# Key norms from the diagonal of k kᵀ, and a triangular substitution on GpSimd instead of VectorE

## The chip, the cores and the metric

The kernel runs on one core of a Trainium2 chip. The metric is the device time of one execution in microseconds (us); the time of a kernel is the median of several runs. A core has five engines with a queue of instructions each: TensorE (PE, with its weight loads shown apart as PEld), VectorE (DVE), ScalarE (ACT), GpSimd (POOL) and SyncE (SP), which here only issues DMAs. SBUF is the on-chip memory with 128 partitions; PSUM is the accumulator memory that TensorE writes.

## The reference

One transformer block with adaptive layer norm, for 8 sequences of 256 tokens with 256 channels. In order: a normalised and modulated input `h`; a gated delta-rule attention with 16 key heads of 128 channels, two value heads for each key head; a gated residual; and a feed-forward layer that keeps the two largest of every four hidden values. What matters here is the attention:

```python
qkv = einsum('btc,dc->btd', x, W_qkv)                 # then a causal convolution over 4 tokens
q = _l2norm(q); k = _l2norm(k)                        # k / sqrt(sum(k*k))
def step(S, inp):                                     # over the 256 tokens
    Sk = einsum('bhi,bhipj->bhpj', k_t, S)
    dv = b_t[..., None] * (v_t - Sk)
    S = S * d_t + einsum('bhi,bhpj->bhipj', k_t, dv)
    o = einsum('bhi,bhipj->bhpj', q_t, S)
```

The recurrence is computed in chunks of 128 tokens. Within a chunk the updates `dv` solve a triangular system whose matrix has the entries k_s·k_t times decay and beta, so the kernel needs the products k kᵀ of a chunk, the squared norms of the keys, and the inverse of a unit triangular 128x128 matrix for each value head and chunk.

## The kernel before

The work is ordered in 16 groups: four pairs of sequences, and in each four groups of four key heads (`groups`, `GH = 4`). While the four heads of one group go through `attend`, the next group is got ready in the background.

For each key head of the coming group `stage_a` makes: the keys `k_t` (two projections on TensorE into `ps_k`, then `convolved`: one ScalarE copy and six VectorE multiply-adds); the squared norms `n2` (`norms2`, line 499: four TensorE transposes of 128x128 into `ps_n2k`, line 447, and four ScalarE squares with a running sum, line 451); from them `rk2` and `bk` on VectorE, and `diag` and `nk` on GpSimd (lines 516 and 523); the products k kᵀ of four chunks into the PSUM bank `ps_kk` (line 532); a scan `e` over 1032 decay entries on VectorE (line 551); and the matrix `a_t` = `ps_kk` times `e` (line 563, two VectorE instructions of 512 elements). The 32x32 diagonal blocks of `a_t` go to DRAM in four DMAs (line 572).

When the four heads of a group are there, `stage_b` loads all their 128 blocks of 32x32 into `blk`, one block in each partition (line 585), and inverts them by substitution: 30 steps of two instructions, a product `tmp` (line 604) and a subtraction from `blk` (line 610), of j·(31−j) elements in step j. Each instruction needs the result of the one before. After step 16 and at the end ScalarE turns the result (lines 592 and 597), which goes to DRAM as `scr_x` and `scr_y`. `levels` loads it again (line 690 and after) and joins the blocks in four rounds of small matmuls (lines 707, 710, 720, 723, 737 to 751) to the 128x128 inverses `t_inv` that `attend` multiplies with (line 804).

`attend` ends with the norm of the output: `ss` on VectorE (line 858), `rs` by a power on GpSimd (line 105), four products `og` (line 871). In the background there are also units of the feed-forward layer, whose selection of two in four is VectorE work (lines 211 to 229).

The order of the instructions on each engine is fixed when the program is built, by a planner that plays the program through with costs of its own and puts on each engine what is ready, in the order in which the code gives it. On the chip each engine then takes its own list strictly in order. `tc.issue_after(ins)` puts the instructions of its block behind `ins` if they run on the same engine; the first group's heads are put behind the last instruction of the first substitution (`first_solved`, lines 1068, 1100 and 1134).

PSUM has eight banks here: three for `ps_in`, two for `ps_inv` (`ps_kk`, the rounds of `levels`, the feed-forward) and three for `ps_mix`.

Of the kernel before, what the change touches and what calls it, by code (L numbers as in the profile page):

```python
# [11 lines left out]
F32 = mybir.dt.float32  # L12
AF = mybir.ActivationFunctionType
ALU = mybir.AluOpType
AX = mybir.AxisListType
# [3 lines left out]
P = 128  # L19
# [29 lines left out]
def adaln_block(  # L49
# [18 lines left out]
    nc = tc.nc  # L68
# [4 lines left out]
    NCH = T // P  # L73
    NK = w_heads.shape[0]
    NV = 2 * NK
    NS = 2 * NCH
# [19 lines left out]
    ident = identx[:, 1:PE1]  # L96
# [269 lines left out]
    with ExitStack() as scope:  # L366
        rec_pool = scope.enter_context(tc.tile_pool(name="rec", bufs=7))
# [73 lines left out]
        def norms2(src, name):  # L441

            n2 = small.tile([P, 2, NCH], F32, tag=name, name=name)
            ps = bank(ps_in if name == "n2k" else ps_in, [P, 2, NCH, P], f"ps_{name}")
            for i in range(2):
                for n in range(NCH):
                    nc.tensor.transpose(ps[:, i, n, :], src[:, i, n * P : (n + 1) * P], ident)
            for i in range(2):
                for n in range(NCH):
                    junk = mixp.tile([P, P], F32, tag="junk", name="junk", bufs=2)  # L450
                    nc.scalar.activation(
                        junk, ps[:, i, n, :], AF.Square, accum_out=n2[:, i, n : n + 1]
                    )
            return n2
# [24 lines left out]
        def stage_a(kh, bp, hp, wk, h_bp, scr):  # L479

            rec = {"kh": kh, "bp": bp, "hp": hp, "h": h_bp}
            first = bp == 0 and kh < GH
            if not first:
                dbc = single.tile([P, 2, NS * PE1], F32, tag="dbc", name="dbc")
                nc.sync.dma_start(
                    out=dbc,
                    in_=d_dram[bp][kh]
# [3 lines left out]
            k_t = rec_pool.tile([P, 2, T], F32, tag="k_t", name="k_t")  # L491
# [4 lines left out]
            else:  # L496
                convolved(k_t, ps, conv_sb[:, kh, 0, :])
            yield rec
            n2 = norms2(k_t, "n2k")
            nc.vector.tensor_scalar_max(n2, n2, L2_EPS2)  # L500
            nk = small.tile([P, 2 * NCH], F32, tag="nk", name="nk", bufs=7)
            rec["nk"] = nk
# [22 lines left out]

            e = rec_pool.tile([P, 2, NS, PE1], F32, tag="e", name="e")
            rec["e"] = e
            ps_kk = bank(ps_inv, [P, 2 * NCH, P], "ps_kk")
            for i in range(2):
                for n in range(NCH):  # L530
                    kc = k_t[:, i, n * P : (n + 1) * P]
                    nc.tensor.matmul(ps_kk[:, i * NCH + n, :], lhsT=kc, rhs=kc, start=True, stop=True)
            if first:
                e_f, diag_f = e.rearrange("p i s t -> p (i s t)"), diag.rearrange("p s t -> p (s t)")
                for c0 in range(0, 2 * NS, 3):
# [26 lines left out]
            for i in range(2):  # L562
                nc.vector.tensor_tensor(
                    out=a_t[:, i].rearrange("p (n h) t -> p n h t", h=2),
                    in0=ps_kk[:, i * NCH : (i + 1) * NCH, None, :].to_broadcast([P, NCH, 2, P]),
                    in1=e[:, i, :, 0:P].rearrange("p (n h) t -> p n h t", h=2),
                    op=ALU.mult,
                )
# [8 lines left out]
        def stage_b(scr, scr_x, scr_y):  # L577

            blk = single.tile([P, Q, Q], F32, tag="blk", name="blk")
            nc.sync.dma_start(out=blk, in_=scr)
            xb = single.tile([P, Q, Q], F32, tag="xb", name="xb")
            nc.gpsimd.memset(blk.rearrange("p a b -> p (a b)")[:, :: Q + 1], -1.0)
            yield

            def turn(rows):  # L590

                nc.scalar.activation(
                    xb[:, rows], blk[:, :, rows].rearrange("p b a -> p a b"), AF.Copy, scale=-1.0
                )
                if rows.stop == Q:
                    nc.sync.dma_start(out=scr_x, in_=xb)
                nc.scalar.activation(blk[:, :, rows], blk[:, :, rows], AF.Copy, scale=-1.0)
                if rows.stop == Q:
                    nc.sync.dma_start(out=scr_y, in_=blk)

            for j in range(1, Q - 1):
                m = Q - 1 - j
                tmp = single.tile([P, j, m], F32, tag="tmp", name="tmp", bufs=2)
                nc.vector.tensor_tensor(  # L604
                    out=tmp,
                    in0=blk[:, j, None, j + 1 :].to_broadcast([P, j, m]),
                    in1=blk[:, 0:j, j, None].to_broadcast([P, j, m]),
                    op=ALU.mult,
                )
                solved = nc.vector.tensor_tensor(  # L610
                    out=blk[:, 0:j, j + 1 :], in0=blk[:, 0:j, j + 1 :], in1=tmp, op=ALU.subtract
                )
# [601 lines left out]
```

## Time and profile before

| | |
|---|---|
| median of 3 runs | 2111.28 us (2106.41 to 2114.01) |
| the profiled execution | 2106.59 us, of which the span from first to last instruction is 2104.6 us |
| TensorE busy | 2000.5 us, 95% of the span |
| VectorE busy | 1666.0 us, 79% |
| ScalarE busy | 1271.3 us, 60% |
| GpSimd busy | 391.1 us, 19% |
| mean granted TensorE clock | 0.991 |

The profile is that of one execution. A group line names the code line, the engine and the operation, the output and the inputs by the program's names, the shapes and the count; then come the total busy time in us, the mean duration of one in ns, and the time in which the engine sat idle just before these instructions, with what ended that idle time. A line of waits reads "who waited <- for whom: us in total, times, longest". Windows give for a stretch of the execution the busy time of each engine. A timeline line starts with the start and the duration in us.

### The profile page before, as it was taken

To read this page: it belongs to the slowest core of one execution; us is meant where nothing else is said; L and a number is where in the kernel's file an instruction comes from. 1 tells how busy PE (TensorE), PEld (TensorE's weight loads), DVE (VectorE), ACT (ScalarE), POOL (GpSimd) and SP (SyncE) were. 2 spreads that over 40 slices of the span, in tenths; PEclk is the share of its full clock that TensorE was granted. 3 is DMA by queue.
4 is the path that set the end of the run, shared out by engine and by line. 5 is a ranking of instruction groups with operands and counts; after the bars stand their busy time and mean duration, and the time that the engine had idled before them with its cause. 6 is when DMAs were issued, how large, how long until landed. Compare 5 with 4: busy or idle time off the path is not lost. (4 is left out here: it accounts for less than half of the span.)

```text
span 2104.6 us, 45727 instructions
## 1 busy us (share of the span) xinstructions
PE 2000.5 (95%) x16684; PEld 1583.3 (75%) x16684; DVE 1666.0 (79%) x4039; ACT 1271.3 (60%) x4260; POOL 391.1 (19%) x376
## 2 busy tenths in 40 slices
PE   8999999899999999999999989999999999999998
PEld 5567777677778777777777777777777877777877
DVE  6778887878788787788878779787978869787557
ACT  3557677766656556566665655657566655656652
POOL 3121312112121211212021121211213121121110
PEclk9999999999999999999999999999999999999999
DMA  4342414333343544434444443443444343344226
GB/s 127 99 131 72 117 55 108 99 80 105 92 115 103 125 115 102 123 105 111 140 92 111 107 123 113 114 115 99 128 110 115 97 127 110 94 121 116 66 91 218
DMA packets 356257, 230.99 MB, mean 110 GB/s; under 512 B 286265, under 2 KB 297913, under 8 KB 356033
## 3 DMA queue, kind: packets, MB, share of 16 engines
q1 hardware_dynamic: 336160, 167.53, 30.7%
q10 hardware_dynamic: 19872, 60.54, 9.3%
q8 instruction: 132, 2.16, 0.4%
q14 instruction: 93, 0.75, 0.1%
HBM read 188.38 MB, written 29.12 MB: 103 GB/s over the span
## 5 line engine op out<-in xcount | busy, mean ns | idle before, releaser
L420 DVE SCALAR_TENSOR_TENSOR cv<-ps_qv,conv_sb,cv 128x510 f32<-128x510 f32 (+2 forms) x564 | 409.4, 739 | 88.1 <-ACT cv L418 84.4
L432 PE MATMUL ps_qv<-h_bp,wh 128*128 128x512 f32 x768 | 365.7, 602 | 8.4 <-DVE cv L420 7.1
L105 POOL TENSOR_TENSOR rs<-ss,minus_halves 128x4 f32<-128x4 f32 x128 | 147.9, 1163 | 942.3 <-DVE ss L858 941.8
L646 PE MATMUL ps_z<-wh,h_bp 128*128 128x256 f32 x1024 | 252.1, 387 | 17.7 <-DVE cv L420 17.2
L901 PE MATMUL ps_y<-wo,og_p 128*128 128x256 f32 x1024 | 236.3, 380 | 2.6 <-ACT gz L653 2.2
L646 PEld LDWEIGHTS ps_z<-wh,h_bp 128*128 128x128 f32 x1024 | 186.9, 193 | 49.1 <-DVE cv L420 22.4
L838 ACT ACTIVATE junk<-o 128x128 f32<-128x128 f32 x512 | 154.2, 305 | 112.1 <-DVE o L854 96.8
L432 PEld LDWEIGHTS ps_qv<-h_bp,wh 128*128 128x128 f32 x768 | 134.3, 193 | 112.7 <-issue 100.2
L901 PEld LDWEIGHTS ps_y<-wo,og_p 128*128 128x128 f32 x1024 | 188.2, 190 | 27.7 <-ACT gz L653 3.3
L604 DVE TENSOR_TENSOR tmp<-blk 128x30 f32<-128x30 f32 (+14 forms) x480 | 156.9, 327 | 56.4 <-DMA blk<-scr 48.7
L418 ACT ACTIVATE cv<-ps_qv,conv_sb 128x512 f32<-128x512 f32 x188 | 129.3, 689 | 107.5 <-PE ps_qv L432 106.8
L516 POOL TENSOR_TENSOR diag<-consts,bk 128x1032 f32<-128x1032 f32 x64 | 123.5, 1929 | 364.5 <-DVE bk L507 329.1
L420 DVE SCALAR_TENSOR_TENSOR k_t<-ps_k,conv_sb,k_t 128x510 f32<-128x510 f32 (+1 forms) x189 | 139.8, 741 | 37.6 <-ACT k_t L418 35.6
L610 DVE TENSOR_TENSOR blk<-blk,tmp 128x30 f32<-128x30 f32 (+14 forms) x480 | 156.8, 327 | 9.6
L551 DVE TENSOR_TENSOR_SCAN e<-dbc,diag 128x1032 f32<-128x1032 f32 x60 | 138.1, 2302 | 19.5 <-POOL diag L516 13.4
L871 DVE SCALAR_TENSOR_TENSOR og<-o,rs,gz 128x128 f32<-128x128 f32 x512 | 145.8, 344 | 8.4 <-POOL rs L105 7.7
L812 PE MATMUL ps_ks<-u,cross 128*128 128x128 f32 x1024 | 141.7, 280 | 7.1 <-ACT u L806 3.9
L812 PEld LDWEIGHTS ps_ks<-u,cross 128*128 128x128 f32 x1024 | 128.7, 193 | 16.6 <-issue 6.3
L190 PE MATMUL ps_ff<-h,w_ff 128*128 128x128 f32 x1024 | 132.5, 277 | 4.2 <-ACT h L149 2.3
L190 PEld LDWEIGHTS ps_ff<-h,w_ff 128*128 128x128 f32 x1024 | 124.4, 192 | 14.9 <-issue 5.9
L778 ACT ACTIVATE vn<-ps_v,nk 128x256 f32<-128x256 f32 x256 | 104.5, 486 | 51.4 <-PE ps_v L773 51.2
L826 ACT ACTIVATE o<-ps_ks,g_in 128x128 f32<-128x128 f32 x256 | 79.9, 365 | 87.2 <-DVE rr L817 78.5
(180 smaller groups left out, 4189.9 us busy)
## 6 DMA issues: line engine op xcount, KB each, us to landing
wh<-in_w_heads ACTq DMA_DIRECT2D x64, 640.0 KB, 4.5
w_ff<-in_w_ff SPq DMA_DIRECT2D x128, 256.0 KB, 3.1
dbc<-d_dram SPq DMA_DIRECT2D x60, 516.0 KB, 3.7
wo<-in_w_heads ACTq DMA_DIRECT2D x32, 512.0 KB, 3.7
w_dn<-in_w_down SPq DMA_DIRECT2D x64, 256.0 KB, 3.0
wk<-in_w_keys SPq DMA_DIRECT2D x16, 512.0 KB, 3.5
scr<-a_t SPq DMA_DIRECT2D x256, 32.0 KB, 2.1
blk<-scr SPq DMA_DIRECT2D x16, 512.0 KB, 4.5
```

The costliest lines, as they stand in the source:

```text
L105: nc.gpsimd.tensor_tensor(out=out, in0=in_, in1=minus_halves[:, :n], op=ALU.pow)
L190: nc.tensor.matmul(ps[:, a, l, :], lhsT=w[:, k, l, :], rhs=h2[:, k, :], start=(k == 0), stop=(k == CC - 1),)
L420: nc.vector.scalar_tensor_tensor(out=dst[:, :, d:], in0=ps[:, :, : T - d], scalar=taps[:, KC - 1 - d : KC - d], in1=dst[:, :, d:], op0=ALU ...
L432: nc.tensor.matmul(ps.rearrange("p b t -> p (b t)"), lhsT=w[k], rhs=h_bp[:, k, :], start=(k == 0), stop=(k == CC - 1),)
L551: nc.vector.tensor_tensor_scan(e.rearrange("p i s t -> p (i s t)"), dbc.rearrange("p i f -> p (i f)"), diag.rearrange("p s t -> p (s t)"), ...
L604: nc.vector.tensor_tensor(out=tmp, in0=blk[:, j, None, j + 1 :].to_broadcast([P, j, m]), in1=blk[:, 0:j, j, None].to_broadcast([P, j, m]), ...
L610: solved = nc.vector.tensor_tensor(out=blk[:, 0:j, j + 1 :], in0=blk[:, 0:j, j + 1 :], in1=tmp, op=ALU.subtract)
L646: nc.tensor.matmul(ps[:, n, :], lhsT=h_bp[:, k, i * T + n * P : i * T + (n + 1) * P], rhs=wh[:, k * 640 + 384 : (k + 1) * 640], start=(k = ...
L812: nc.tensor.matmul(ps_ks[:, ct, h, :], lhsT=cross[:, h, ct, :], rhs=u0[:, h, :], start=True, stop=True)
L838: nc.scalar.activation(junk, o[:, n, h, :], AF.Square, accum_out=ss[:, n, h : h + 1])
L871: nc.vector.scalar_tensor_tensor(out=og[:, n, h, :], in0=o[:, n, h, :], scalar=rs[:, 2 * n + h : 2 * n + h + 1], in1=gz[:, i, n, h, :], op ...
L901: nc.tensor.matmul(ps_y[:, n, :], lhsT=og_p[:, j // 2, i, n, j % 2, :], rhs=wo[:, j // 2, j % 2, :], start=(j == 0), stop=(j == 3),)
```

## The change

Three parts, all in the background work:

- The squared norms of the keys are read from the diagonal of k kᵀ. The four products into `ps_kk` are made right behind the keys; ScalarE copies all of `ps_kk` to SBUF (`kk`, the odd half of the tile `a_t`, 512 elements for each partition); VectorE multiplies it with the identity into the even half and sums each row of 128 by a `tensor_reduce`. The four transposes and four squares for each key head fall away.
- `a_t` is then made from `kk` in SBUF instead of from PSUM, as two instructions by value head instead of by sequence, still 512 elements each. The second one writes over `kk` itself.
- The 60 instructions of each substitution run on GpSimd instead of VectorE. With that `first_solved` is a GpSimd instruction.

```diff
@@ stage_a
-            n2 = norms2(k_t, "n2k")
+            ps_kk = bank(ps_inv, [P, 2 * NCH, P], "ps_kk")
+            for i in range(2):
+                for n in range(NCH):
+                    kc = k_t[:, i, n * P : (n + 1) * P]
+                    nc.tensor.matmul(ps_kk[:, i * NCH + n, :], lhsT=kc, rhs=kc, start=True, stop=True)
+            a_t = rec_pool.tile([P, 2, NS, P], F32, tag="a_t", name="a_t", bufs=6)
+            rec["a"] = a_t
+            a_h = a_t.rearrange("p i (n h) t -> p (i n) h t", h=2)
+            kk, diagonal = a_h[:, :, 1], a_h[:, :, 0]
+            nc.scalar.copy(kk, ps_kk)
+            n2 = small.tile([P, 2, NCH], F32, tag="n2k", name="n2k")
+            nc.vector.tensor_tensor(
+                out=diagonal, in0=kk, in1=ident[:, None, :].to_broadcast([P, 2 * NCH, P]), op=ALU.mult
+            )
+            nc.vector.tensor_reduce(
+                out=n2.rearrange("p i n -> p (i n)"), in_=diagonal, axis=AX.X, op=ALU.add
+            )
...
-            ps_kk = bank(ps_inv, [P, 2 * NCH, P], "ps_kk")
...
-            a_t = rec_pool.tile([P, 2, NS, P], F32, tag="a_t", name="a_t", bufs=6)
-            rec["a"] = a_t
-            for i in range(2):
-                nc.vector.tensor_tensor(
-                    out=a_t[:, i].rearrange("p (n h) t -> p n h t", h=2),
-                    in0=ps_kk[:, i * NCH : (i + 1) * NCH, None, :].to_broadcast([P, NCH, 2, P]),
-                    in1=e[:, i, :, 0:P].rearrange("p (n h) t -> p n h t", h=2),
-                    op=ALU.mult,
-                )
+            e_h = e[:, :, :, 0:P].rearrange("p i (n h) t -> p (i n) h t", h=2)
+            for h in range(2):
+                nc.vector.tensor_tensor(out=a_h[:, :, h], in0=kk, in1=e_h[:, :, h], op=ALU.mult)
@@ stage_b
-                nc.vector.tensor_tensor(
+                nc.gpsimd.tensor_tensor(
                     out=tmp,
...
-                solved = nc.vector.tensor_tensor(
+                solved = nc.gpsimd.tensor_tensor(
                     out=blk[:, 0:j, j + 1 :], in0=blk[:, 0:j, j + 1 :], in1=tmp, op=ALU.subtract
```

More of the change, by code (lines that the diff above doesn't have):

```diff
@@ L527, in stage_a @@
             rec["e"] = e
-            ps_kk = bank(ps_inv, [P, 2 * NCH, P], "ps_kk")
-            for i in range(2):
-                for n in range(NCH):
-                    kc = k_t[:, i, n * P : (n + 1) * P]
-                    nc.tensor.matmul(ps_kk[:, i * NCH + n, :], lhsT=kc, rhs=kc, start=True, stop=True)
             if first:
@@ L559, in stage_a @@
             yield rec
-            a_t = rec_pool.tile([P, 2, NS, P], F32, tag="a_t", name="a_t", bufs=6)
-            rec["a"] = a_t
-            for i in range(2):
-                nc.vector.tensor_tensor(
-                    out=a_t[:, i].rearrange("p (n h) t -> p n h t", h=2),
-                    in0=ps_kk[:, i * NCH : (i + 1) * NCH, None, :].to_broadcast([P, NCH, 2, P]),
-                    in1=e[:, i, :, 0:P].rearrange("p (n h) t -> p n h t", h=2),
-                    op=ALU.mult,
-                )
+            e_h = e[:, :, :, 0:P].rearrange("p i (n h) t -> p (i n) h t", h=2)
+            for h in range(2):
+                nc.vector.tensor_tensor(out=a_h[:, :, h], in0=kk, in1=e_h[:, :, h], op=ALU.mult)
             a_f = a_t.rearrange("p i s t -> p (i s) t")
```

## The prediction

> **What bounds the kernel now.** I read the page's busy table first, then windows along one group, then the groups by shape, the waits, and the timeline around the substitution.
>
> ```profile
> PE 2000.5 (95%) x16684; PEld 1583.3 (75%) x16684; DVE 1666.0 (79%) x4039; ACT 1271.3 (60%) x4260; POOL 391.1 (19%) x376
> ...
> L604 DVE TENSOR_TENSOR tmp<-blk 128x30 f32<-128x30 f32 (+14 forms) x480 | 156.9, 327 | 56.4 <-DMA blk<-scr 48.7
> ...
> L610 DVE TENSOR_TENSOR blk<-blk,tmp 128x30 f32<-128x30 f32 (+14 forms) x480 | 156.8, 327 | 9.6
> ```
>
> TensorE is busy for all but 104 us of the span: it is the bound on the whole. The substitution (L604, L610) is 314 us of VectorE. One group of 122.6 us in the middle, cut into before, during and after its substitution (columns: sum, then PE, PEld, DVE, ACT, POOL busy):
>
> ```profile
> 1086.60:1128.80 42.20, 41.48 (x373) 32.63 (x372) 35.62 (x68) 25.17 (x95) 14.40 (x11) 1.00 0.51 134
> 1128.80:1170.60 41.80, 38.53 (x265) 32.23 (x264) 40.40 (x125) 23.94 (x82) 6.09 (x7) 1.00 0.32 92
> 1170.60:1209.20 38.60, 38.60 (x372) 29.04 (x372) 24.37 (x52) 25.52 (x79) 5.12 (x5) 1.00 0.47 119
> ```
>
> The middle row is the point: during the substitution VectorE is full (40.4 of 41.8) and TensorE loses 3.3 us, most of what it loses in the group. The list of waits agrees:
>
> ```profile
> DVE tmp L604 <- DMA blk<-scr: 48.7, 16, 7.0
> ...
> PE ps_z L646 <- DVE cv L420: 17.2, 15, 3.0
> ...
> PE ps_qv L432 <- DVE cv L420: 7.1, 7, 2.5
> PE ps_w L707 <- DMA x_even<-scr_x: 3.2, 3, 2.0
> ```
>
> VectorE stands 3 us a group in front of L604 until `blk` lands, and TensorE waits 24.3 us in all for convolutions that VectorE brings late. For the result of the substitution (`x_even`) it hardly waits.
>
> **The norms.**
>
> ```profile
> L451 ACT ACTIVATE junk<-ps_n2k 128x128 f32<-128x128 f32 x256 | 69.3, 289 | 60.4 <-PE ps_n2k L447 60.3
> ...
> L563 DVE TENSOR_TENSOR a_t<-ps_kk,e 128x512 f32<-128x512 f32 x128 | 81.9, 681 | 0.6
> ...
> L447 PE MATMUL ps_n2k<-consts,k_t 128*128 128x128 f32 x256 | 39.2, 276 | 1.2 <-ACT k_t L418 0.9 <-DVE k_t L420 0.3
> ```
> ```profile
> 1202.27 0.60 PE L447 MATMUL ps_n2k<-consts,k_t 128*128 128x128 f32 x4
> ```
>
> Four transposes take 0.60 us, one alone 0.276, so one more takes (0.60−0.276)/3 = 0.108 us of TensorE. 256 of them removed is 27.6 us at the pitch, 39.2 us by busy time. TensorE being the bound, I take 27.6 in full. ScalarE drops 256 squares (69 us and their accumulator reads) and gains 64 copies of 512 elements at about 0.69 us (as L418), 44 us: no bound before or after. VectorE gains a product (0.68, as L563) and a row sum, which no row shows; a copy of 512 elements from PSUM takes 0.679 us (L910), and I bound the sum by 0.4 (the 256-element statistics of L131) and 2.3 us (the 1032-element scan L551) and take 0.68, since cost here goes by elements read. 64 x 1.36 = 87 us against 314 us that leave: VectorE ends near 1440 us, 68%. In the chain from keys to `diag` 1.36 us of VectorE and a copy of 0.7 us replace four squares of some 0.29: under 1 us later for each head, covered by 40 us of other background work. `a_t` from SBUF keeps 512 elements; L169, both inputs in SBUF, takes 421 ns for 256, and PSUM-fed L198 413, so 0 us. `ps_kk` gives its bank back after the copy instead of after the scan, which can only help `levels` and the feed-forward; 0 to −5 us, I take 0. `a_t` is held from the norms on; six buffers, and the earlier hold is a scan long, 0.
>
> **The substitution on GpSimd.** No row shows it there; the nearest are these.
>
> ```profile
> L516 POOL TENSOR_TENSOR diag<-consts,bk 128x1032 f32<-128x1032 f32 x64 | 123.5, 1929 | 364.5 <-DVE bk L507 329.1 <-DVE e L551 11.1 <-DVE mv L132 10.4
> ...
> L657 POOL TENSOR_SCALAR eps_q<-n2q 128x4 f32<-128x4 f32 x64 | 24.8, 387 | 70.4 <-ACT junk L451 66.9
> ...
> L1012 POOL TENSOR_TENSOR taps<-consts,conv_sb 128x512 f32<-128x512 f32 x1 | 1.0, 1041 | 4.3 <-DMA conv_sb<-in_conv_w 4.3
> ```
>
> Undisturbed, L516 takes 1.917 us. With L1012 that gives 1.685 ns an element and 0.18 us fixed. The 30 steps have sum j(31−j) = 4960 elements, twice: 9920 x 1.685 ns + 60 x 0.18 = 27.4 us. A dependent instruction starts 0.04 us (VectorE's steps) to 0.1 us (`ss` to `rs`) after its source: +2.4 to +6, so 30 to 33; with L657's mean 0.387 as the fixed part it is 45. Into the same queue come 4 `rs` (1.16 each) and 2 `eps_q`: 5.4 us.
>
> Then the two engines disturb each other:
>
> ```profile
> 1363.39 2.48 DVE L229 SCALAR_TENSOR_TENSOR hid<-mag,hid 128x384 f32<-128x384 f32 x2
> ```
> ```profile
> 1363.58 2.14 POOL L516 TENSOR_TENSOR diag<-consts,bk 128x1032 f32<-128x1032 f32 x1 [3.87 <-DVE bk L507]
> ```
> ```profile
> L871 DVE SCALAR_TENSOR_TENSOR og<-o,rs,gz x512: 318/344/353, 137.0 to 2044.0; 128x128 f32<-128x128 f32 x171
> ```
>
> A VectorE instruction with both tensors in SBUF stood until `diag` was through (the quickest L229 takes 0.27), and `diag` itself started its data 0.22 us late behind the first. `og`, beside `rs` in many places, never exceeds 353 ns, so four-element powers hold nothing. In the window above the timeline has 40 such VectorE instructions besides the substitution, 13.9 us. GpSimd meets one in a third of cases for half of 0.35 us: 60 x 0.33 x 0.17 = 3.4 us. VectorE loses 40 x 0.75 x 0.14 = 4 us and has 19.7 us freed. So: 33 + 5.4 + 3.4 = 42 us against 41.8 now. The result is there when it is now; ends 36 and 54. I take 0, since L516 and L1012 are the same operation and L657 is another. What VectorE no longer does late is worth half of TensorE's 24.3 us: −12 (ends 0 and −24).
>
> Two rules of the Trainium skill speak against the change. "GPSIMD Engine Reference", Elementwise — side-by-side cycle accounting, has 2.6 cycles an element at 1.2 GHz, 2.17 ns where the rows give 1.685; by it the substitution is an estimated 4.8 us longer a group and the kernel near 2140. "SBUF — State Buffer", Who interferes with whom, lets whoever is first hold the shared port for the whole instruction; L516 agrees and L871 beside `rs` doesn't, and by the rule VectorE would lose an estimated 7 us a group instead of 4.
>
> **Start.** The first substitution runs undisturbed now, from 60.6 to 83.8 us, 23.2 us; on GpSimd 30 to 36 (45 at the outside). But the first heads' VectorE work, which line 1100 queued behind it, is now free of it. Ends 0 and +13, I take +5. `eps_q` of the first heads does queue behind it; `ss`, its only reader, comes after `levels` anyway.
>
> **Sum.** 2106.6 (the profiled execution) − 27.6 − 12 + 5 = 2072. Its time is 4.7 us under the median of 2111.3, so 2077.
>
> **Rivals.**
> Slower, the substitution arrives late. TensorE's order is fixed, and it comes to L707 just as `x_even` lands:
>
> ```profile
> 1174.74 1.82 SPq L690 DMA_DIRECT2D x_even<-scr_x  x4
> ```
> ```profile
> 1177.67 0.24 PE L707 MATMUL ps_w<-x_even,a_t 32*32 32x32 f32 x2
> ```
>
> 2.9 us with 2.3 us to landing (the DMA's median) leave 0.6 us. Every us that the planner does not know of costs 15 us over the groups; also the 3 us late `blk`, which VectorE absorbs now, would reach TensorE here. From 0.6 + 34/15 = 2.9 us a group the gain is gone. At 54 us instead of 42, half of it unplanned, it is (6−0.6) x 15 = 81 us: 2158. Against it: 12 waits of `og` for `rs` in 128 say that GpSimd's times are planned about right.
> Less: VectorE's port losses eat the relief, −12 becomes 0: 2089.
> No change: `t_inv` is used within about 4 us of being made, so the chain keys, substitution, `levels`, `attend` may set the 122 us and TensorE's saved time turns into idle time: 2111.
>
> **How the numbers follow.** Forecast 0.46, less 0.07, no change 0.07, late substitution 0.40. What can be told from no change is about 0.3%, 6 us. Faster is 0.46 + 0.07 = 0.53, same 0.07, slower 0.40. The likeliest case by itself spans 2047 (39.2 and 24 saved, nothing at the start) to 2097. The range takes in 2158 and a little more, leaving out the longer substitutions.
>
> **What would show it.** Right: TensorE's busy time falls by 28 to 39 us, the transposes of `ps_n2k` are gone, GpSimd's substitution pairs average near 0.46 us, VectorE in that stretch drops under 30 of 42 us, waits for DVE `cv` shrink, L707 still hardly waits. Wrong: L707 or L804 waits for `x_even` or ScalarE's `t_inv` by several us a group, or substitution instructions above 0.6 us.

## The result, and the profile after

The change makes the kernel slower. Median 2194.53 us (2193.74 to 2196.92, four runs) against 2112.65 us for the kernel before in the same session: a ratio of 1.0395, 95% interval 1.0371 to 1.0419. (A ratio here can differ by 0.1% from the quotient of the two medians.) The forecast was 2077 us, with a range to 2165; the sign is wrong and the time is outside the range. The profiled execution took 2196.92 us with a span of 2195.1.

From the page of the changed kernel, the busy times and three of the costliest groups (columns as before):

```profile
PE 2024.9 (92%) x16428; PEld 1589.9 (72%) x16428; DVE 1572.9 (72%) x3207; ACT 1245.7 (57%) x3813; POOL 882.9 (40%) x1336
...
L615 POOL TENSOR_TENSOR blk<-blk,tmp 128x30 f32<-128x30 f32 (+14 forms) x480 | 256.1, 534 | 35.4
L609 POOL TENSOR_TENSOR tmp<-blk 128x30 f32<-128x30 f32 (+14 forms) x480 | 244.7, 510 | 34.9 <-issue 0.2
...
L876 DVE SCALAR_TENSOR_TENSOR og<-o,rs,gz 128x128 f32<-128x128 f32 x512 | 193.3, 437 | 82.6 <-POOL rs L105 81.9
```

256 transposes are gone (16684 TensorE instructions have become 16428), and yet TensorE is busy for 24 us longer and idle for 2195.1 − 2024.9 = 170 us instead of 104. VectorE has 93 us less to do. Neither engine with less work has made the kernel faster.

The same cut of one group in the middle as before the change: the 42.2 us ahead of a substitution, the substitution, and 38.6 us behind it (columns: sum, then PE, PEld, DVE, ACT, POOL busy, the granted clock, the DMA share and GB/s).

```profile
1133.40:1175.60 42.20, 39.01 (x366) 29.13 (x365) 35.17 (x65) 22.38 (x71) 12.51 (x12) 0.96 0.53 144
1175.60:1218.20 42.60, 38.16 (x234) 32.49 (x233) 28.72 (x64) 20.95 (x75) 36.50 (x67) 0.96 0.25 78
1218.20:1256.80 38.60, 36.49 (x352) 27.52 (x351) 24.29 (x48) 25.98 (x74) 2.43 (x3) 0.96 0.46 114
```

In the middle row VectorE has fallen from 40.4 us to 28.7, and the substitution takes 42.6 us where it took 41.8. But in the first row, where the norms are made, VectorE has what it had before (35.2 us), and TensorE now loses 3.2 us there instead of 0.7, 4.4 instead of 3.3 in the middle and 2.1 instead of none behind. The granted clock, 1.00 in all three rows before, is 0.96.

The waits, in the order of the list (who waits <- for whom: us in total, times, longest):

```profile
DVE cv L420 <- ACT cv L418: 145.8, 50, 8.1
...
DVE og L876 <- POOL rs L105: 81.9, 38, 7.2
ACT xb L597 <- POOL blk L615: 76.3, 26, 9.9
...
PE ps_u L809 <- DVE aq L799: 34.4, 24, 3.8
...
PE ps_w L712 <- DMA x_even<-scr_x: 19.1, 11, 4.1
...
PE ps_kq L790 <- DVE o L859: 17.4, 6, 4.5
...
PE ps_qv L432 <- DVE cv L420: 9.8, 4, 3.1
```

In the kernel before, the first three were these; `xb` then waited for VectorE's last steps:

```profile
DVE cv L420 <- ACT cv L418: 84.4, 46, 4.5
...
ACT xb L592 <- DVE blk L610: 13.0, 8, 3.4
...
DVE og L871 <- POOL rs L105: 7.7, 12, 1.2
```

TensorE waits for `aq` and `o`, VectorE's steps inside `attend`, 52 us in all (4.2 before), where it used to wait for convolutions.

Where the 90.5 us between the two spans lie can be added up. The trace records every stretch in which TensorE was granted half its clock: 38 us within the span before, 147 us after, so 19 and 73 us of full-speed time lost, of which 17.6 and 67.9 lie in TensorE's busy time. TensorE's busy time at full clock is then 2000.5 − 17.6 = 1982.9 before and 2024.9 − 67.9 = 1957.0 after. So: 25.9 us of work saved, 66.1 us of idle time and 50.3 us of half clock added: +90.5. The idle time and the half clock are the large terms. The work is known less well: the runs below with the same 16428 TensorE instructions come out between 1944 us (d4) and 1978 (n1) by this reckoning.

One place shows how both arise. VectorE in the changed kernel (timeline: start, duration, then the instruction):

```profile
1152.91 0.69 DVE L573 TENSOR_TENSOR a_t<-a_t,e 128x512 f32<-128x512 f32 x1
...
1153.58 0.69 DVE L510 TENSOR_TENSOR a_t<-a_t,consts 128x512 f32<-128x512 f32 x1
1154.18 0.69 DVE L573 TENSOR_TENSOR a_t<-a_t,e 128x512 f32<-128x512 f32 x1
...
1155.10 0.68 DVE L513 TENSOR_REDUCE n2k<-a_t 128x4 f32<-128x512 f32 x1
...
1155.90 0.74 DVE L420 SCALAR_TENSOR_TENSOR cv<-ps_qv,conv_sb,cv 128x510 f32<-128x510 f32 x1
...
1157.41 0.68 DVE L799 TENSOR_TENSOR aq<-ps_kq,e 128x512 f32<-128x512 f32 x1
```

and TensorE there:

```profile
1151.91 1.88 PE L432 MATMUL ps_qv<-h_bp,wh 128*128 128x512 f32 x4
...
1158.15 0.74 PE L809 MATMUL ps_u<-vn,t_inv 128*128 128x128 f32 x4 [3.04 <-DVE aq L799]
1158.70 3.58 PE L432 MATMUL ps_qv<-h_bp,wh 128*128 128x512 f32 x4
```

The products that `aq` reads were through at 1152.1 us. `aq` runs at 1157.4, and VectorE, busy nearly all the while, takes the new product (L510) and row sum (L513) among others before it. TensorE, in its fixed order, waits 3.04 us. Then it pays again: four products of 512 columns that took 1.88 us before the gap take 3.58 us after it. Windows over the same place:

```profile
1136.00:1155.00 19.00, 18.85 (x220) 14.94 (x220) 18.33 (x35) 10.27 (x33) 8.07 (x8) 1.00 0.57 156
1155.00:1158.30 3.30, 0.26 (x3) 0.15 (x2) 3.27 (x9) 0.37 (x1) 0.66 (x1) 1.00 0.36 69
1158.30:1161.60 3.30, 3.30 (x8) 1.74 (x9) 3.30 (x4) 0.37 (x1) 2.23 (x2) 0.56 0.25 50
1161.60:1165.00 3.40, 3.40 (x19) 2.62 (x17) 3.31 (x6) 1.75 (x5) 0.00 (x0) 0.93 0.47 143
```

VectorE is full in all four rows (18.3 of 19.0 us, then 9.9 of 10.0), and the clock falls to 0.56 in the row behind the gap.

### The profile page after: what moved, and what is told of

Its sections match the earlier page's. It is cut to its first block, busy times and chain, and to the rows that moved or that the text cites. A ratio compares the mean times of both kernels' runs of the same rounds, so it can differ in the third digit from the quotient of the medians.

```text
span 2195.1 us, 44788 instructions
## 1 busy us (share of the span) xinstructions
PE 2024.9 (92%) x16428; PEld 1589.9 (72%) x16428; DVE 1572.9 (72%) x3207; ACT 1245.7 (57%) x3813; POOL 882.9 (40%) x1336
## 4 chain that ended last, share of the span: by engine, by line
DVE 28%; PE 27%; POOL 19%; DMA 12%; issue 6%; ACT 5%; SPq 2%; ACTq 0%; DVEq 0%; POOLq 0%
POOL blk L615 8%; POOL tmp L609 7%; DVE cv L420 5%; DVE e L562 4%; PE ps_qv L432 4%; DVE og L876 3%; DVE a_t L573 3%; PE ps_z L651 3%; DMA blk<-scr 3%; DMA scr<-a_t 3%; PE ps_y L906 2%; PE ps_ks L817 2%; DMA x_even<-scr_x 2%; PE ps_k L432 2%; POOL rs L105 2%
## 5 line engine op out<-in xcount | busy, mean ns | idle before, releaser
L420 DVE SCALAR_TENSOR_TENSOR cv<-ps_qv,conv_sb,cv 128x510 f32<-128x510 f32 (+1 forms) x564 | 408.3, 739 | 151.0 <-ACT cv L418 145.8
L432 PE MATMUL ps_qv<-h_bp,wh 128*128 128x512 f32 x768 | 383.4, 626 | 12.8 <-DVE cv L420 9.8
L105 POOL TENSOR_TENSOR rs<-ss,minus_halves 128x4 f32<-128x4 f32 x128 | 134.2, 1053 | 475.2 <-DVE ss L863 473.1
L615 POOL TENSOR_TENSOR blk<-blk,tmp 128x30 f32<-128x30 f32 (+14 forms) x480 | 256.1, 534 | 35.4
L609 POOL TENSOR_TENSOR tmp<-blk 128x30 f32<-128x30 f32 (+14 forms) x480 | 244.7, 510 | 34.9 <-issue 0.2
L876 DVE SCALAR_TENSOR_TENSOR og<-o,rs,gz 128x128 f32<-128x128 f32 x512 | 193.3, 437 | 82.6 <-POOL rs L105 81.9
L432 PEld LDWEIGHTS ps_qv<-h_bp,wh 128*128 128x128 f32 x768 | 139.5, 201 | 124.5 <-issue 115.2
L651 PEld LDWEIGHTS ps_z<-wh,h_bp 128*128 128x128 f32 x1024 | 192.4, 196 | 44.4 <-issue 14.8
L817 PEld LDWEIGHTS ps_ks<-u,cross 128*128 128x128 f32 x1024 | 133.5, 199 | 17.3 <-issue 7.8
L822 DVE SCALAR_TENSOR_TENSOR rr<-ps_ks,g_ex,vn 128x128 f32<-128x128 f32 x256 | 77.0, 342 | 66.8 <-PE ps_ks L817 66.8
```

What stands on the lines that cost most here:

```text
L105: nc.gpsimd.tensor_tensor(out=out, in0=in_, in1=minus_halves[:, :n], op=ALU.pow)
L420: nc.vector.scalar_tensor_tensor(out=dst[:, :, d:], in0=ps[:, :, : T - d], scalar=taps[:, KC - 1 - d : KC - d], in1=dst[:, :, d:], op0=ALU ...
L432: nc.tensor.matmul(ps.rearrange("p b t -> p (b t)"), lhsT=w[k], rhs=h_bp[:, k, :], start=(k == 0), stop=(k == CC - 1),)
L609: nc.gpsimd.tensor_tensor(out=tmp, in0=blk[:, j, None, j + 1 :].to_broadcast([P, j, m]), in1=blk[:, 0:j, j, None].to_broadcast([P, j, m]), ...
L615: solved = nc.gpsimd.tensor_tensor(out=blk[:, 0:j, j + 1 :], in0=blk[:, 0:j, j + 1 :], in1=tmp, op=ALU.subtract)
L651: nc.tensor.matmul(ps[:, n, :], lhsT=h_bp[:, k, i * T + n * P : i * T + (n + 1) * P], rhs=wh[:, k * 640 + 384 : (k + 1) * 640], start=(k = ...
```

## The experiments

The main runs in one table; the others stand with their ratios where they come up. The planner orders every one of these programs anew, so each run differs from its neighbour by its edit and by what the planner made of it. "Idle" is TensorE's, span less busy time; "half clock" is the full-speed time lost within the span in the stretches granted half the clock. Both are of the profiled execution; ratios are against the kernel before on the same chip, with the 95% interval.

| run | what differs | median us | ratio | idle | half clock |
|---|---|---|---|---|---|
| before | | 2108 to 2113 | | 104 | 19 |
| after | | 2194.5 | 1.0395 (1.0371–1.0419) | 170 | 73 |
| e1 | norms' part alone | 2186.1 | 1.0369 (1.0345–1.0394) | 181 | 58 |
| e2 | substitution's part alone | 2140.5 | 1.0143 (1.0126–1.0161) | 123 | 38 |
| d2 | e1 without product and row sum | 2111.6 | 1.0018 (1.0002–1.0035) | 128 | 39 |
| d1 | after without product and row sum | 2152.0 | 1.0200 (1.0172–1.0228) | 145 | 60 |
| l1 | d2, product and row sum unread | 2148.8 | 1.0178 (1.0136–1.0219) | 146 | 48 |
| t1 | before without transposes, squares | 2094.7 | 0.9922 (0.9903–0.9940) | 108 | 27 |
| v1 | before, norms by one-column products | 2150.3 | 1.0177 (1.0154–1.0201) | 107 | 43 |
| s3 | e2, first on VectorE, both queues clear | 2111.1 | 1.0007 (0.9996–1.0018) | 108 | 33 |
| d4 | after, both queues clear, no norm work | 2127.8 | 1.0095 (1.0078–1.0112) | 135 | 51 |

### The two parts by themselves

e1 puts the substitution back on VectorE (lines 609 and 615), e2 is the kernel before with these two lines on GpSimd.

```diff
@@ e2, against before (e1, against after, is the reverse)
-                nc.vector.tensor_tensor(
+                nc.gpsimd.tensor_tensor(
                     out=tmp,
...
-                solved = nc.vector.tensor_tensor(
+                solved = nc.gpsimd.tensor_tensor(
```

> The norms from the diagonal as in the changed kernel, the substitution left on VectorE as before. Theory Q (the loss is the substitution on GpSimd: it runs behind the place that the planner gave it, and ScalarE at its turn of the blocks and VectorE at the products that need the power on GpSimd stand in their queues): 2070 to 2090 us, 27.6 us of TensorE less and up to 10 us of idle time less, granted clock at 0.99. Theory N (the loss is the norms: copy, product and row sum come later than four squares, and hold up the scan): 2150 to 2195 us. Theory P (the loss is the SBUF port shared by VectorE and GpSimd): 2070 to 2095 us.

> The substitution on GpSimd as in the changed kernel, the norms by transposes and squares as before. Theory Q: 2195 to 2230 us, the changed kernel's loss with the 28 us of transposes back. Theory N: 2095 to 2125 us, near the kernel before. Theory P: 2195 to 2230 us.

e1 took 2186.1 us, in theory N's range and far outside Q's and P's; e2 took 2140.5, outside all three. Both parts lose by themselves: the norms 78 us, the substitution 32. Together they lose 82 to 86, so they share some of it. The larger loss is in the part whose VectorE cost the prediction had set against VectorE time saved elsewhere; with the substitution still on VectorE, e1 has no such saving, and VectorE is busy for 1767 us. TensorE stands up to 9.8 us for `xn`, a normalised input that VectorE brings late:

```profile
PE 2009.1 (92%) x16428; PEld 1584.0 (72%) x16428; DVE 1767.5 (81%) x4167; ACT 1241.8 (57%) x3811; POOL 405.5 (19%) x376
```
```profile
PE ps_h L147 <- DVE xn L137: 24.0, 4, 9.8
```

The traces also show in which stretch TensorE loses. Its idle time and the half clock in its busy time, added up within the fifteen substitutions behind the first and between them, are 38 and 60 us before, 59 and 125 us in e1, 75 and 49 us in e2, 64 and 132 us in the changed kernel. So the norms lose mostly between the substitutions, where their work stands (neither in e1 nor in the changed kernel does a product or row sum on VectorE start within one of these fifteen); the moved substitution loses within itself.

### Smaller suspects: a bank, a buffer, and load alone

n1 is e1 with `ps_kk` in the other PSUM pool; b1 is before with `a_t` taken early, the key squares written into it; b2 is before with five idle products of 128x128 on VectorE for each head; VectorE's busy time rises by 74 us (1740.0 against 1666.0).

```diff
@@ n1, against e1
-            ps_kk = bank(ps_inv, [P, 2 * NCH, P], "ps_kk")
+            ps_kk = bank(ps_in, [P, 2 * NCH, P], "ps_kk")
@@ b2, against before, behind norms2
+            for r in range(5):
+                load = single.tile([P, P], F32, tag="load", name="load")
+                nc.vector.tensor_tensor(out=load, in0=k_t[:, r % 2, 0:P], in1=ident, op=ALU.mult)
```

> The norms alone (substitution on VectorE), with ps_kk in one of the three banks of ps_in, where the transposes had theirs, instead of one of the two of ps_inv, which the rounds of levels and the feed-forward need. Norms alone in ps_inv took 2186 us. Theory B (the loss of the norms is the PSUM bank): 2085 to 2130 us. Theory A (it is the buffer of a_t, one of six, held from the norms on instead of from behind the scan): 2175 to 2195 us. Theory D (it is 87 us more on VectorE, in the queue where the convolutions and the scan stand): 2175 to 2195 us.

> The kernel before, norms by transposes and squares, but the squares of the keys are written into a_t (they went into a scratch tile), so a_t's buffer is taken at the norms as in the change; no operation is added. Theory A: 2150 to 2195 us. Theory B: 2100 to 2120 us, as before. Theory D: 2100 to 2120 us.

> The kernel before with five more products of 128x128 in SBUF on VectorE for each key head, right behind the norms, written to a scratch tile that nobody reads: 320 x 0.28 = 90 us more of VectorE, as much as the change's product and row sum, and in the same place. Theory D: 2150 to 2190 us. Theory A: 2100 to 2125 us. Theory B: 2100 to 2125 us.

n1: 2178.7 us, ratio 1.0335 (1.0296–1.0373): some 7 us of e1's 78 go with the other bank, and the two intervals overlap. b1: 2113.3 us, 1.0022 (1.0001–1.0044): the earlier hold of `a_t` costs about 5 us. b2: 2149.4 us, 1.0194 (1.0153–1.0234), just under theory D's range: these 74 us of VectorE work whose result nobody reads, put where the norms are made, cost 41 us, although VectorE in the kernel before is busy for only 79% of the span. That pointed at the amount of VectorE work in this place.

### The norms: how much is work, how much is the chain

d1 (against after) and d2 (against e1) replace product and row sum by one instruction of four elements, which leaves out the norms of the keys. l1 is d2 with both put back behind `bk`, into a tile that nobody reads. d3 is after with the product alone on GpSimd.

```diff
@@ d1, d2
-            nc.vector.tensor_tensor(
-                out=diagonal, in0=kk, in1=ident[:, None, :].to_broadcast([P, 2 * NCH, P]), op=ALU.mult
-            )
-            nc.vector.tensor_reduce(
-                out=n2.rearrange("p i n -> p (i n)"), in_=diagonal, axis=AX.X, op=ALU.add
-            )
+            nc.vector.tensor_scalar(n2.rearrange("p i n -> p (i n)"), kk[:, :, 0], 0.0, 1.0, ALU.mult, ALU.add)
@@ l1, against d2, behind bk
+            nc.vector.tensor_tensor(
+                out=diagonal, in0=kk, in1=ident[:, None, :].to_broadcast([P, 2 * NCH, P]), op=ALU.mult
+            )
+            nc.vector.tensor_reduce(
+                out=n2x.rearrange("p i n -> p (i n)"), in_=diagonal, axis=AX.X, op=ALU.add
+            )
@@ d3, against after
-            nc.vector.tensor_tensor(
+            nc.gpsimd.tensor_tensor(
                 out=diagonal, in0=kk, in1=ident[:, None, :].to_broadcast([P, 2 * NCH, P]), op=ALU.mult
```

> The changed kernel, with the product by the identity and the row sum (1.36 us of VectorE for each head by my prediction, 87 us in all) replaced by one VectorE instruction of four elements that reads the copied products; the norms of the keys are left out with it. The earlier products k k^T, ScalarE's copy, the wait of VectorE for that copy and the substitution on GpSimd all stay. Theory D (the loss is the work that the norms put on VectorE in the stretch where it stands between keys and attend): 2105 to 2130 us. Theory O (the loss is the order and the extra hop keys, TensorE, ScalarE, VectorE, not the amount of work): 2165 to 2195 us.

> The kernel with the norms' part of the change alone (substitution on VectorE), with the same product and row sum replaced by one VectorE instruction of four elements; the norms of the keys are left out with it. With both it takes 2186 us. Theory D (VectorE's added work): 2075 to 2105 us, which would be at or under the kernel before, since the transposes and squares are gone too. Theory O (order and hop): 2150 to 2185 us.

> The changed kernel with the product by the identity on GpSimd, the row sum still on VectorE: some 44 us of VectorE work go, and GpSimd, which has the substitutions, gets about 1 us more for each head ahead of diag. Theory D: 2150 to 2180 us, part of the loss goes with the work. Theory O: 2190 to 2205 us, since there is one more hop.

> The kernel with the norms' part alone, the norms themselves replaced by one VectorE instruction of four elements (2112 us without the work), and the product by the identity and the row sum made after bk, into a tile that nobody reads: the same work in VectorE's queue, but not in the chain from keys to diag. Theory W (the amount of VectorE's work there counts, wherever it stands): 2165 to 2195 us. Theory C (the work counts because diag and the scan wait for it): 2112 to 2135 us. Between them: both.

d2 took 2111.6 us and d1 2152.0. Both lie outside the ranges written down: d2 is 6.6 us over theory D's and 38 under O's, d1 lies between the two, 22 us over D's and 13 under O's. The product and the row sum are worth 74.5 us without the substitution's move and 42.5 with it. d3 took 2184.4 us, ratio 1.0353 (1.0326–1.0380), just over D's range: moving half of the work to GpSimd brings some 10 us. l1, 2148.8 us, splits the 74.5 in two: 37 us come with the same work standing unread in VectorE's queue, another 37 when it stands ahead of `diag` and the scan, which wait for its result. That fits b2 (41 us). The split is rough, since l1's four runs spread from 2138.9 to 2159.8 us.

The page's busy line of d2, to be held against e1's above:

```profile
PE 1979.4 (94%) x16428; PEld 1566.5 (74%) x16428; DVE 1698.8 (81%) x4103; ACT 1243.6 (59%) x3809; POOL 398.7 (19%) x376
```

VectorE's busy time differs by 69 us, about what b2 added, its share is 81% in both, and the time differs by 74.5 us. The share says nothing here.

### What TensorE's saved time is worth

d2 has no transposes and no norms' work, and still takes what the kernel before takes. t1 takes only the transposes and squares away; v1 makes the norms otherwise, with one ScalarE square and four products with a column of ones.

```diff
@@ t1, against before
-            n2 = norms2(k_t, "n2k")
+            n2 = small.tile([P, 2, NCH], F32, tag="n2k", name="n2k")
+            nc.vector.tensor_scalar(n2, k_t[:, :, 0:NCH], 0.0, 1.0, ALU.mult, ALU.add)
@@ v1, against before
-            n2 = norms2(k_t, "n2k")
+            e = rec_pool.tile([P, 2, NS, PE1], F32, tag="e", name="e")
+            sq = e.rearrange("p i s t -> p (i s t)")[:, : 2 * T]
+            nc.scalar.activation(sq, k_t.rearrange("p i t -> p (i t)"), AF.Square)
+            ps_n = bank(ps_in, [P, 2, NCH], "ps_n2k")
+            for i in range(2):
+                for n in range(NCH):
+                    c0 = (i * NCH + n) * P
+                    nc.tensor.matmul(ps_n[:, i, n : n + 1], lhsT=sq[:, c0 : c0 + P], rhs=ones_col, start=True, stop=True)
```

> The kernel before, with the four transposes into ps_n2k and the four squares with their running sums taken away for each key head, and one VectorE instruction of four elements in their place; the norms of the keys are left out with them. Theory T (TensorE, busy for 95% of the span, is the bound, and what it does less of is saved): 28 us less, 2075 to 2090 us. Theory H (the order on VectorE and the chain from keys to attend set the length of a group, and TensorE's saved time turns into idle time): 2095 to 2112 us.

> The kernel before, with the norms made in another way: one ScalarE square of all 512 columns of the keys, written into the tile that the scan will use, and four TensorE products of the squared keys with a column of ones, which give the norms in PSUM, where VectorE takes them. No work is added to VectorE; ScalarE has one instruction of about 0.69 us instead of eight of 1.95 us together; TensorE has four products of one column instead of four transposes. Theory T: 2080 to 2100 us. Theory H: 2100 to 2115 us.

t1 gains 15.8 us, a ratio of 0.9922, between the two theories' ranges. TensorE's work at full clock falls from 1982.8 to 1956.2 us, close to the 27.6 us predicted; 4 us of it become idle time and 8 us are lost to half clock. So while VectorE's work stays what it was, three fifths of TensorE's saving are kept. d2, 17 us over t1, has the rest of the norms' part: the hop through ScalarE's copy, the earlier hold of `ps_kk` and `a_t`, and `a_t` from SBUF, 99.0 us where the same 128 products from PSUM took 81.9. These were not separated.

v1 was to be a better kernel and is not: 2150.3 us, over both theories' ranges. Its trace says part of why:

```profile
1009.53 0.95 PE L508 MATMUL ps_n2k<-ones_col,e 128*128 128x1 f32 x8
```
```profile
PE 2041.9 (95%) x16940; PEld 1622.6 (75%) x16940; DVE 1668.3 (78%) x4040; ACT 1246.4 (58%) x3811; POOL 380.7 (18%) x376
```

Four products with a single column are eight TensorE instructions, each with a weight load of 128x128, and take 0.95 us where four transposes took 0.60, 22 us over 64 heads. TensorE's busy time rises by 41 us and the span by 44.6, with idle time as before (107 us). About half of the 41 us is work at full clock, the other half is more half clock; what brought that on, at the same idle time, was not found. v1 also takes the buffer of `e` earlier, which was not tested by itself.

### The substitution: two queues behind it

In e2 VectorE, GpSimd and TensorE show this (three pieces of the timeline):

```profile
904.25 0.16 DVE L858 SCALAR_TENSOR_TENSOR ss<-ss,eps_q 128x4 f32<-128x4 f32 x1 [0.82 <-ACT junk L838]
911.47 2.88 DVE L871 SCALAR_TENSOR_TENSOR og<-o,rs,gz 128x128 f32<-128x128 f32 x4 [7.05 <-POOL rs L105]
914.26 1.52 DVE L420 SCALAR_TENSOR_TENSOR cv<-ps_qv,conv_sb,cv 128x510 f32<-128x510 f32 x2
915.70 0.41 DVE L854 TENSOR_TENSOR o<-o,ps_o 128x256 f32<-128x256 f32 x1
```
```profile
904.40 0.56 POOL L604 TENSOR_TENSOR tmp<-blk 128x210 f32<-128x210 f32 x1
...
909.85 0.61 POOL L604 TENSOR_TENSOR tmp<-blk 128x238 f32<-128x238 f32 x1
910.42 1.02 POOL L105 TENSOR_TENSOR rs<-ss,minus_halves 128x4 f32<-128x4 f32 x1
```
```profile
916.16 1.22 PE L785 MATMUL ps_kq<-cv,k_t 128*128 128x256 f32 x2 [4.91 <-DVE o L854]
```

`ss` is there at 904.4 us. `rs` stands behind nine more instructions of the substitution in GpSimd's list and runs at 910.4. VectorE stands 7.05 us in front of `og`, with the convolution and `o` of the next head queued behind it, and TensorE waits 4.91 us for that `o`. The other queue is ScalarE's: `xb`, the turn, waits for GpSimd's last steps, and what ScalarE has behind it waits too:

```profile
ACT xb L592 <- POOL blk L610: 72.4, 23, 7.1
```

The following runs take these queues away, or put the first substitution back (s2). The reciprocal leaves out the square root in `rs`.

```diff
@@ e3 (against after), s1 (against e2)
-            rsqrt(rs, ss.rearrange("p n h -> p (n h)"))
+            nc.vector.reciprocal(rs, ss.rearrange("p n h -> p (n h)"))
@@ e4 (against after)
-                nc.scalar.activation(
-                    xb[:, rows], blk[:, :, rows].rearrange("p b a -> p a b"), AF.Copy, scale=-1.0
+                nc.gpsimd.tensor_scalar_mul(
+                    xb[:, rows], blk[:, :, rows].rearrange("p b a -> p a b"), -1.0
...
-                nc.scalar.activation(blk[:, :, rows], blk[:, :, rows], AF.Copy, scale=-1.0)
+                nc.gpsimd.tensor_scalar_mul(blk[:, :, rows], blk[:, :, rows], -1.0)
@@ s2 (against e2), the first group
-            for done in stage_b(scr, *scratch):
+            for done in stage_b(scr, *scratch, eng=nc.vector):
@@ s3: s2 with the edits of e3 and e4;  e5: after with them;  d4: d1 with them
```

> The changed kernel, with rs made on VectorE by a reciprocal instead of the power on GpSimd; this leaves out the square root, so the output's scale is another; it takes 128 powers of 1.05 us out of GpSimd's queue and 128 reciprocals of 0.17 us go to VectorE. Theory Q: the 82 us that VectorE stands in front of og go, and with them part of TensorE's idle time and of the half clock: 2135 to 2175 us. Theory N: 2185 to 2200 us, no change to the changed kernel. Theory P: 2185 to 2200 us, since og still meets the substitution at the port (437 ns mean for one stays).

> The changed kernel, with the four turns of the blocks (xb and blk, 512 elements each) on GpSimd behind the substitution instead of on ScalarE. Theory Q: the 76 us that ScalarE stands for them go; GpSimd gets 4 x 0.6 to 1 us longer in each group, so x_even lands 2 to 3 us later: 2150 to 2200 us. Theory N: 2190 to 2235 us, the longer chain alone. Theory P: 2195 to 2235 us, since GpSimd reads SBUF for longer.

> The kernel with the substitution alone on GpSimd (2140 us), with rs made by a VectorE reciprocal, the square root left out. The wait of og for rs, 91 us of VectorE idle time there, goes. Theory R (the loss of the substitution's move is rs standing behind substitution steps in GpSimd's queue): 2100 to 2120 us. Theory S (it is the schedule around the substitution and VectorE's relief is of no use where it comes): 2130 to 2142 us.

> The kernel with the substitution alone on GpSimd (2140 us), but the first group's substitution on VectorE as before; the other fifteen stay on GpSimd. Theory A (the start: the first substitution has nothing beside it, and its extra 12 us between the first two loads of blk are lost one to one): 2126 to 2132 us. Theory B (the first group's heads, queued behind it on VectorE, win as much as it loses): 2136 to 2145 us.

> The same, with the two waits that stand behind the substitution in a queue taken away as well: rs is a VectorE reciprocal (the square root is left out) and the two turns of each half of the result are GpSimd instructions behind the steps instead of ScalarE's. Theory Q (the rest of the 32 us is these two queues, each of which hides the other): 2100 to 2115 us. Theory S (VectorE's relief comes where TensorE does not wait for it, and the rest is the changed order): 2120 to 2135 us.

One at a time the queues bring little: on the changed kernel `rs` alone gives e3 2179.8 us (ratio 1.0342, 1.0322–1.0361), the turn alone e4 2198.8 (1.0425, 1.0407–1.0444); on e2 `rs` alone gives s1 2145.2 (1.0155, 1.0136–1.0175), no better than e2. e3 lies between two theories' ranges, s1 just over theory S's. s1 spoke against the queue, and I had half given it up. s2 says that the start is not it either: 2139.5 us (1.0149, 1.0129–1.0169), though the first substitution is back to 23.2 us from 37.3. s3 settles it: with both queues clear the kernel takes 2111.1 us, 28 us less than s2 and the same as the kernel before. What is left in s3 is

```profile
PE 2001.5 (95%) x16684; PEld 1590.6 (75%) x16684; DVE 1529.1 (72%) x3267; ACT 1229.9 (58%) x4194; POOL 812.8 (39%) x1212
```

a VectorE with 137 us less to do, a TensorE idle for 108 us, and no gain. The moved substitution costs what its queues cost, and what VectorE's relief brings is lost again: within the fifteen substitutions TensorE loses 17 us to idle time and half clock instead of 38, between them 97 instead of 60. One of the waits that grew there is for the result of the substitution itself (3.2 us before):

```profile
PE ps_w L707 <- DMA x_even<-scr_x: 22.0, 11, 3.8
```

What the rest of the 37 us is was not separated. Whether the turn alone, on e2, would do the same was not run.

### Both causes together

> The changed kernel with both queues behind the substitution taken away: rs a VectorE reciprocal (the square root is left out) and the turns GpSimd instructions. Theory Q+ (the queues cost 28 us whatever else is there, the norms' part 54 to 75 us): 2155 to 2175 us. Theory M (with the norms' work on VectorE, the queues no longer matter by themselves, since VectorE is late anyway): 2178 to 2195 us.

> The same, with the product by the identity and the row sum replaced by one VectorE instruction of four elements (the norms are left out too). Theory Q+ (these three are the whole loss): 2095 to 2125 us. Otherwise 2130 us or more, and something of the change is still unnamed.

e5 took 2161.2 us, ratio 1.0247 (1.0228–1.0266): on the changed kernel too the two queues are worth 31 (by the ratios) to 33 us, and not less because VectorE is late. d4 took 2127.8, 33 us less again and just over its range. The two causes are 65 to 67 of the change's 82 to 86 us; 18 us over the kernel before stay unnamed. d4 still has the first substitution on GpSimd, and d2's hop and copy; how the 18 us divide among them and the new order of the queues was not separated.

## Why the prediction was wrong, step by step

**The bound.** "TensorE being the bound, I take 27.6 in full." The size fits: TensorE's work at full clock fell by 25.9 us in the change and 26.7 in t1. But t1 kept 15.8 of it, and d2 none. 95% busy meant that little else was late in the old order, not that nothing would be in a new one. The rival "no change" had this mechanism, and at 0.07 it was too cheap.

**The norms on VectorE: the step that failed.** The term was 1.36 us a head, "87 us against 314 us that leave: VectorE ends near 1440 us, 68%", and nothing for the chain, "covered by 40 us of other background work". The durations were fair (row sum 0.678 us, as taken; product 0.682 in the median, 0.862 in the mean). The place was not. The 314 us leave the stretch of the substitution, the 87 us arrive in the stretch where keys, scans and `attend` share VectorE, and there it has spells without a free place (18.3 of 19.0 us, then 9.9 of 10.0, in the windows above). This term, taken at 0, measured +75 us alone and +43 beside the moved substitution: about half by the amount (l1, b2), about half because `diag` and the scan hang on it (l1 against e1). My own window of before gave VectorE 35.6 of 42.2 us in that stretch; I read it only for the middle row.

**VectorE's total.** 1440 predicted, 1572.9 measured. What VectorE loses beside GpSimd was what I gave it: in e2 the durations of all VectorE instructions, added up, fell by 251 us instead of 314, so the others grew by 62 us, predicted 4 a group or 64. The 1440 left this loss out, though it was costed by itself. It also took durations from a busy time in which overlapping instructions count once: the busy time of e2 fell by 196 us only.

```profile
PE 2015.9 (94%) x16684; PEld 1591.2 (74%) x16684; DVE 1470.4 (69%) x3079; ACT 1272.8 (60%) x4260; POOL 863.5 (40%) x1336
```

Smaller is that one `a_t` from SBUF takes 759 ns in the mean instead of 681 (taken at 0), and the product 55.2 us in all instead of 43.5.

**The substitution's time.** Right: 42 us predicted, 41.7 in the mean of fifteen groups (42.7 before). But the sum came out by two errors that cancel: one instruction averages 0.49 us if the quickest of each size is taken, 0.50 in the first group and 0.52 over all, where 0.46 was taken for the computation. By those of the first group an element costs 1.8 to 2.0 ns, not 1.685, so 60 of them, each starting 0.08 us behind the last, make 34.7 us where the sum had 33; the disturbance came to 7.0 us where it had 8.8. The late substitution that I built on such longer times, the forecast's main rival at 0.40, was the wrong reason for the right sign: TensorE waits 19.1 us for `x_even` in the changed kernel (3.2 before), and 22.0 in s3, which takes no longer than the kernel before.

**The queue on GpSimd: the second failed step.** I counted the four `rs` among the substitution's steps as 1.16 us each of GpSimd's time, and took 12 waits of `og` in 128 as a sign that the order was planned about right. I did not ask who stands behind a waiting `og`. It now waits 38 times and 81.9 us, and `xb` on ScalarE, whose wait for GpSimd I did not name at all, 76.3. Together these two are 28 us (s2 to s3) or 31 to 33 (after to e5); with only one of them gone little is won (e3, e4, s1).

**The relief, −12.** Waits for convolutions did shrink (`ps_z` from 17.2 to 3.8 us, while `ps_qv` rose from 7.1 to 9.8), the only part of this term that came true. Waits for `aq`, `o` and `x_even` came in their stead, and s3 puts the net worth of the relief, with what came in its stead, at 0, the upper end that I had given.

**The start, +5.** The first substitution went from 23.2 to 36.1 us, the upper end of the bounds. Giving that back in s2 changed the time by 1 us. So this +5 cost nothing that can be seen.

**The clock.** Not in the prediction at all: 50 of the 90 us are idle time's aftermath, TensorE at half clock behind the gaps.

## What to carry to other kernels

An engine's busy share cannot be credited in one stretch and debited in another: ask in which stretch the work leaves and in which it arrives, and what the engine's fixed order has queued behind it there. When a long dependent sequence moves to a quiet engine, list every short instruction that already lives in that engine's queue, and the engines that stand still for them; here clearing one of two such queues won little, clearing both won 28 to 33 us. And to learn what a suspected cost is worth, leave the work out, and then put it back where nobody reads it: the two runs together separate amount from place, as far as the order of the rest stays the same.

## What the hardware showed that I had not expected

**Half clock behind short gaps.** TensorE's clock falls to half for 3.4 us or a multiple of it, and a gap of well under 3.4 us is enough. Over the traces of all twenty kernels here, from 60 us on, I counted TensorE's gaps by length and looked whether a half-clock stretch began within 6.8 us of the gap's start: 97 of 100 gaps of 3.5 us or more, 50 of 59 from 3.0 to 3.5, 46 of 64 from 2.5 to 3.0, 70 of 112 from 2.0 to 2.5, 53 of 150 from 1.5 to 2.0, and 87 of 620 from 0.7 to 1.5 (some of these by chance, or by another gap close by). The Trainium skill, "TensorE: Matmul & The Clock Gate", HAM oscillation — how this bites in real kernels, gives the rule that gaps over about 3.4 us are to be avoided; in these runs gaps of 2 us already do it more often than not. Gaps that lie alone show the same: of those from 2.0 to 2.5 us that began at full clock, with at most 0.6 us of other idle time from 3.4 us before to 6.8 us after their start, 49 of 84 were followed by half clock. These stretches start on a grid of 3.41 us in each trace (all 362 of them from 60 us on), and cut along that grid the traces show plainly what goes before them: at full clock, a window in which TensorE was idle for 60% or more was followed by half clock in 253 of 253 cases, from 50 to 60% in 68 of 108, under 40% in 7 of 11145. Several short gaps in one window do it too: of the windows idle for half or more whose gaps were each under 2 us, 58 of 67 were followed by half clock. A gap so costs its length and, where the clock falls, half of 3.4 us or of a multiple of it.

**One column is not cheap.** An f32 product of 128x128 with one column is two TensorE instructions, and eight in a row take 0.95 us (v1). One such product so costs about twice what a transpose of 128 columns costs (0.108 us at the pitch). The number of columns hardly counts: eight instructions of 128 columns take 1.04 us (`ps_v` in e2, at 908 us).

**Long and short GpSimd instructions.** `og` beside GpSimd's `rs` never exceeded 353 ns before the change, and I took it that short GpSimd instructions hold nothing. Beside the substitution's steps, which read and write up to 240 elements, four `og` took 2.88 us in e2 instead of 1.4, and their mean rose from 344 to 437 ns in the changed kernel.
